# A graph layer on one core: two slots change places, the start's TensorE work lies at the head of the loop, and the first turn turns its own x

## The chip, the cores and the metric

The kernel runs on one core of a Trainium2 chip. The metric is the device time of one execution in microseconds, median of several runs. TensorE (PE, with its weight loads as PEld), VectorE (DVE), ScalarE (ACT), GpSimd (POOL) and SyncE (SP, which issues most transfers) each run their own list of instructions in order and wait for each other by semaphores.

## The reference

Inputs: 12,500 nodes of 128 numbers (`x`), 412,500 edges of 48 numbers, sorted by the node they point at (`dst`), one graph vector of 64 and a two-layer network. Cut to what is computed:

```python
agg = jax.ops.segment_sum(edge_attr_48, dst, num_segments=12500)
h = jnp.maximum(_layernorm(x, axis=-1), 0.0)
c = jnp.concatenate([h, agg, u], axis=1)          # 128 + 48 + 64; u is the same row for all nodes
y = x + jax.nn.relu(c @ W1 + b1) @ W2 + b2
```

So for each node the edges that point at it are added up, and a small network is run on node, sum and graph vector. All is float32.

## The kernel before

**The work.** A chunk is 128 x 6 edges, a group four chunks (3,072 edges). A turn of the loop takes eleven groups and 1,024 nodes, which are two halves A and B of 512; there are twelve turns, and a rest behind the loop. The edges of a turn lie in six slots (`SLOTS`, line 39) of one or two groups, each with its own tile `e`, its one-hots `oh`, its sums `ss` and its places `pl`. Per slot VectorE compares the ids within a chunk with 0 to 27 (`onehots`, line 769), TensorE multiplies edges by these one-hots (`add_up`, line 810: `su`, 24 products per group, two matmuls each in the trace) into bank S0 or S1, ScalarE copies the sums out (`ss`), and TensorE adds them to the turn's nodes by a second one-hot (`place`, line 825: `pc`, banks ax and ay). ScalarE copies these out as `ags`.

**The network.** In the next turn the sums meet their nodes: `layer_e` (ha, line 893) adds `ags` x W1 to what `layer_x` (hh, line 888) of the turn before left in four banks (pt, po, ph0, ph1), ScalarE applies relu (hi), and `second` (w2, line 910) multiplies by W2, which VectorE adds to the held x (ho). `hh` needs the normed, transposed x: VectorE takes statistics (`stats`, `variance`), ScalarE a square root (`root`, sq), VectorE finishes `sc` and `sh`, ScalarE makes xn (`norm`, eight activations), TensorE transposes (`turn`, tu), ScalarE copies (hT). So in turn i the statistics and norms of the x of turn i+1 are made, and that x is transposed in turn i+1. An x tile is loaded again when it has been normed and copied into `hold`. Results are kept in `hold` and stored behind the loop.

**The order.** Nothing schedules at run time: `prologue`, `body` and `epilogue` write operations into a list, `Flow.order` derives the waits from what each reads and writes, and each engine runs its own in the written order. SyncE issues loads in that order too, and blocks where a slot is still being read. In the first turn what belongs to a turn before is left out (`f.skip`).

**TensorE's code.** For the other engines the start is straight code ahead of a loop. For TensorE `Flow.run` writes one loop by hand and puts the start's work inside, in a branch behind the code of the turn. A counter `j` tells where to go. Before, in round 1 it branches from the head over `if0` and `if1` to `work0` (ids: five `of`, ten triples of transposes `td`), in round 2 over `if0` to `work1` (transposes of the first x, `su5` for the rows ahead of the first turn, `bi`, and `hh` of the first x), and in round 3 the first turn begins. In the text's listing a row's xN counts products of the program.

**The start.** SyncE loads two of five pieces of dst, both halves of x, the other pieces, then e and weights. VectorE turns ids into differences (`dst_1`, lines 677 to 681, three buffers), TensorE transposes them (`dst_2`, line 694), ScalarE copies them to `rel` (line 695).

Of the kernel before, what the change touches and what calls it, by code (L numbers as in the profile page):

```python
# [10 lines left out]
F32 = mybir.dt.float32  # L11
# [7 lines left out]
P = 128  # L19
# [19 lines left out]
SLOTS = [(1, 6), (2, 7), (3, 8), (4, 9), (5,), (10, 11)]  # L39
NS = len(SLOTS)  # L40
HI = 64

# [12 lines left out]
class Flow:  # L55
# [146 lines left out]
    def run(self):  # L202
# [96 lines left out]
        pe.reg_add(j, j, 1)  # L299
        either(n, "if0", "first", "IS_GE")  # L300
        part("first", "head", False)
        at, k = "first", 0
        for skip, some in groupby(own, lambda o: o["name"] in self.skip):
            some = list(some)
            if not skip:
                for o in some:
                    repeat(o, None)
                continue
            part(f"if{k}", at if k else "head")
            at = f"if{k}"  # L310
            either(n + 1, f"brief{k}", f"whole{k}", "IS_GE")
            part(f"whole{k}", at, False)
            for o in some:
                repeat(o, None)
            pe.br(f"pe_both{k}")
            part(f"brief{k}", at, False)
            if k:
                either(2, "work0", "brief1a")
                work(0, "brief1", todo[:most])
# [3 lines left out]
            else:  # L323
                either(2, "if1", "brief0a", "IS_GE")
                part("brief0a", "brief0", False)
                either(n, "work1", "both0")
                work(1, "brief0a", todo[most:])
            part(f"both{k}", at, False)
            at = f"both{k}" if k else "if0"
            k += 1  # L330
# [3 lines left out]
        part("after", "if1", False)  # L334
# [159 lines left out]
def kernel(  # L494
# [106 lines left out]
    mf = [const.tile([P, P // CG], F32, name=f"mf{k}") for k in range(NB)]  # L601
# [70 lines left out]
    def dst_1(b):  # L672
        rows, n, g0 = dst_shape(b)
        d = di[b]
        k = f"di{b}"
        src = [k] + ([k + "r", k + "s"] if b == NB - 1 else [])
        op("DVE", f"fc{b}", src, [f"fc{b}"], lambda i: [nc.vector.tensor_copy(fc[b][:rows], d[:rows, 0:1])])
        k = b % DF
        op("DVE", f"df{b}", src + [f"fc{b}"], [f"df{k}"], lambda i: [
            nc.vector.tensor_scalar(df[k][:rows], d[:rows], fc[b][:rows], (V - 1) / 2, OP.subtract, OP.subtract)])  # L680
        op("DVE", f"mf{b}", [f"fc{b}", "m4"], [f"mf{b}"], lambda i: [nc.vector.tensor_scalar(mf[b][:rows], m4[:rows], fc[b][:rows], None, OP.mult)])

    def dst_2(b):
        rows, n, g0 = dst_shape(b)
        ob, ok = agg[0], "of"
        op("PE", f"of{b}", [f"mf{b}", "aq"], [ok], lambda i: [
            nc.tensor.matmul(ob[:, g0:g0 + n], aq[:rows].rearrange("c k n -> c (k n)"), mf[b][:rows, :n], start=True, stop=True, skip_group_check=True)])
        dv = df[b % DF].rearrange("c (p t) -> c t p", t=T)
        rv = rel[:, :, b * P:b * P + rows]
        for t0 in range(0, T, 3):  # L690
            key, bk = (("PT", pt), ("PH0", ph[0]), ("PO", po))[(2 * b + t0 // 3) % 3]
            pv = bk[:, :3 * P].rearrange("p (t c) -> p t c", t=3)
            op("PE", f"td{b}.{t0}", [f"df{b % DF}", "ident"], [key],
               lambda i, t0=t0, pv=pv: [nc.tensor.transpose(pv[:, t, :rows], dv[:rows, t0 + t, :], ident[:rows, :rows]) for t in range(3)])
            op("ACT", f"cd{b}.{t0}", [key], [f"rel{b}.{t0}"], lambda i, t0=t0, pv=pv: [nc.scalar.copy(rv[:, t0:t0 + 3], pv[:, :, :rows])])  # L695

# [146 lines left out]
    def stats(k):  # L843
        op("DVE", f"st{k}", [f"x{k}"], [f"st{k}"], lambda i: [nc.vector.bn_stats(st[:, k * R + r], xt[k][:, r]) for r in range(R)])  # L844
# [32 lines left out]
    def turn(k, bk, key, front=""):  # L877
        pv = bk.rearrange("p (r c) -> p r c", r=R)
        op("PE", f"tu{front}{k}", [f"xn{k}", "ident"], [key], lambda i: [nc.tensor.transpose(pv[:, r], xn[k][:, r], ident) for r in range(R)])  # L879
        op("ACT", f"hT{front}{k}", [key], [f"hT{k}"], lambda i: [nc.scalar.copy(hT[k], pv)])  # L880
# [24 lines left out]
    def layers(fn, front=""):  # L905

        for a, k, key, bk in middle:
            fn(f"{front}{k}.{a}", key, bk.rearrange("p (r c) -> p r c", r=R), k, a)
# [36 lines left out]
    def prologue():  # L945
        f.at = -1
        load_dst(0)
        load_dst(1)
        for k in (A, B):
            load_x(k, 1, "SP")  # L950
        for b in range(2, NB):
            load_dst(b)
        load_dst(NB - 1, True)
        dma("SP", "le5.1", [], ["e5.1"], e[5][:, CG:], edge_attr[:GE].rearrange("(c p t) d -> p c (t d)", p=P, t=T))
        load_e(0, 1, 0)
        dma("SP", "lw1h", [], ["w1h"], w1h, W1[0:D])
        load_e(0, 1, 1)
# [5 lines left out]
        for s in range(2, NS):  # L963
# [6 lines left out]
            out=ident, in_=ident, compare_op=OP.not_equal, fill=1.0, base=0, pattern=[[-1, P]], channel_multiplier=1), ["ident"])  # L970
        pool("s5z", ["ssf"], lambda: nc.gpsimd.memset(ssf[:, 0], 0.0))
# [28 lines left out]
        dst_1(0)  # L1000
        dst_2(0)
        dst_1(1)
        stats(A)
        stats(B)
        variance()
        root()
        dst_2(1)
        dst_1(2)
        shift()
        norm(A, (0, 1))  # L1010
        dst_2(2)
        norm(A, (2, 3))
        dst_1(3)
        dst_2(3)
        norm(B, (0, 1))
        dst_1(4)
        dst_2(4)
        norm(B, (2, 3))
# [8 lines left out]
        op("ACT", "ssf", ["bk1"], ["ssf", "bk1"], lambda i: [nc.scalar.copy(ssf[:, 1], agg[1][:, :DE])])  # L1027
        fetch(1)
        onehots(0)
        onehots(1)  # L1030
        op("PE", "bi", ["w1u", "u", "u1", "b1"], ["of"], lambda i: [
            nc.tensor.matmul(agg[0][:, NG + a:NG + a + 1], w1u[:, a * P:(a + 1) * P], u, start=True, stop=True, skip_group_check=True) for a in range(NH)])
        layers(layer_x, "f")
# [3 lines left out]
        onehots(2)  # L1037
# [12 lines left out]
    def body(it):  # L1050
# [30 lines left out]
        norm(A, (0, 1))  # L1081
        turn(B, po, "PO")
        norm(A, (2, 3))
# [7 lines left out]
        layers(layer_x)  # L1091
        onehots(4)
# [62 lines left out]
    f.cut = "tuf0"  # L1155
    f.skip = {f"{n}{k}.{a}" for n in ("ha", "hi", "hh") for k in (A, B) for a in range(NH)} | {f"{n}{k}" for n in ("tu", "hT", "w2", "ho") for k in (A, B)}
# [38 lines left out]
```

## Time and profile before

| | |
|---|---|
| time, median of 3 runs (range) | 265.36 us (264.72 to 265.43) |
| the profiled execution, its span | 266.01 us, 264.1 us |
| busy: TensorE, VectorE, ScalarE | 236.4, 227.9, 132.8 us |
| moved | 94.40 MB, mean 357 GB/s |
| first matmul; first turn of the loop; second turn | 9.78; 28.66; 49.46 us |
| end of the last turn; of the span | 245.92; 264.1 us |

In a row of a timeline stand the start, the length, the engine, the line and operation, what is written and read, how often, and in brackets the idle time before it and what ended it; "issue" means that the profile shows nothing it waited for. A row of windows gives a stretch, its length, the busy time of each engine with its instructions, the granted TensorE clock (1.00 is full), the busy share of the DMA engines and GB/s. A row of a DMA queue gives packets, MB and its share of 16 engines' time. A turn here is always a pass through the loop's body.

### The profile page before, as it was taken

To read this page: it belongs to the slowest core of one execution; us is meant where nothing else is said; L and a number is where in the kernel's file an instruction comes from. 1 tells how busy PE (TensorE), PEld (TensorE's weight loads), DVE (VectorE), ACT (ScalarE), POOL (GpSimd) and SP (SyncE) were. 2 spreads that over 40 slices of the span, in tenths; PEclk is the share of its full clock that TensorE was granted. 3 is DMA by queue.
4 is the path that set the end of the run, shared out by engine and by line. 5 is a ranking of instruction groups with operands and counts; after the bars stand their busy time and mean duration, and the time that the engine had idled before them with its cause. 6 is when DMAs were issued, how large, how long until landed. Compare 5 with 4: busy or idle time off the path is not lost.

```text
span 264.1 us, 17108 instructions
## 1 busy us (share of the span) xinstructions
PE 236.4 (90%) x7537; PEld 184.6 (70%) x7538; DVE 227.9 (86%) x548; ACT 132.8 (50%) x315; POOL 4.3 (2%) x18
## 2 busy tenths in 40 slices
PE   0589922999999999999999999999999999999991
PEld 0575612886796778867967877679679677886780
DVE  5598695799998998998989989989999899899951
ACT  2291115375572673754736826537467367375520
POOL 6000000000000000000000000000000000000000
PEclk9985885899999999999999999999999999999999
DMA  6999999899999999999999999999999999969922
GB/s 209 345 344 386 347 382 384 255 382 390 365 390 393 377 390 392 390 390 392 390 392 391 391 392 391 390 392 390 392 390 390 392 390 390 367 248 380 358 96 76
DMA packets 79545, 94.40 MB, mean 357 GB/s; under 512 B 3228, under 2 KB 72842, under 8 KB 79528
## 3 DMA queue, kind: packets, MB, share of 16 engines
q1 hardware_dynamic: 76318, 88.60, 94.4%
q10 hardware_dynamic: 3114, 5.52, 5.5%
q8 instruction: 10, 0.16, 0.3%
q0 software_dynamic: 96, 0.07, 0.1%
q14 instruction: 7, 0.06, 0.1%
HBM read 87.77 MB, written 6.40 MB: 357 GB/s over the span
## 4 chain that ended last, share of the span: by engine, by line
PE 85%; issue 6%; DVE 3%; ACT 2%; DMA 2%; SPq 0%
PE s L815 28%; PE ph L914 16%; PE ph L891 8%; PE ax L837 7%; PE pt L896 4%; PE pt L891 4%; PE po L891 4%; PE ph L896 4%; PE pt L879 2%; PE po L879 2%; DMA holda<-in_dst_dram 2%; PE ax L801 1%; DVE far L709 1%; ACT rel L695 1%; ACT xnb L868 1%
## 5 line engine op out<-in xcount | busy, mean ns | idle before, releaser
L761 DVE TENSOR_TENSOR oh<-iota_v,rel_i 128x1344 f32<-128x1344 f32 (+1 forms) x78 | 110.9, 1438 | 11.1 <-PE s L815 10.7
L815 PEld LDWEIGHTS s<-e,oh 128*28 128x28 f32 x6336 | 71.0, 108 | 29.2 <-issue 28.6
L815 PE MATMUL s<-e,oh 128*28 128x48 f32 x6336 | 76.2, 208 | 10.8 <-issue 10.8
L819 ACT COPY ss<-s 128x96 f32<-128x96 f32 (+1 forms) x72 | 17.0, 236 | 63.8 <-PE s L815 62.7
L767 DVE TENSOR_SCALAR pl<-iota_w,off_i 128x186 f32<-128x186 f32 x112 | 26.5, 315 | 0.5
L868 ACT ACTIVATE xna<-xa,sh,sc 128x128 f32<-128x128 f32 x52 | 25.7, 494 | 1.3 <-issue 0.4
L868 ACT ACTIVATE xnb<-xb,sh,sc 128x128 f32<-128x128 f32 x52 | 25.5, 490 | 1.3
L914 PE MATMUL ph<-w,hida 128*128 128x128 f32 x192 | 23.5, 276 | 0.0
L914 PEld LDWEIGHTS ph<-w,hida 128*128 128x128 f32 x192 | 22.4, 192 | 0.3 <-issue 0.3
L914 PE MATMUL ph<-w,hidb 128*128 128x128 f32 x176 | 21.4, 275 | 0.0
L914 PEld LDWEIGHTS ph<-w,hidb 128*128 128x128 f32 x176 | 20.5, 192 | 0.0
L837 PE MATMUL ax<-pl,ss 128*48 128x186 f32 (+1 forms) x120 | 20.1, 316 | 0.0
L837 PE MATMUL ay<-pl,ss 128*48 128x186 f32 (+1 forms) x120 | 20.1, 316 | 0.0
L837 PEld LDWEIGHTS ax<-pl,ss 128*48 128x48 f32 x120 | 14.1, 126 | 3.8
L844 DVE BATCH_NORM_STATS2 st<-xa 128x6 f32<-128x128 f32 x52 | 11.3, 285 | 4.2 <-DMA xa<-in_x_dram 4.2
L837 PEld LDWEIGHTS ay<-pl,ss 128*48 128x48 f32 x120 | 14.1, 126 | 0.0
L896 PE MATMUL po<-ags,w1a 48*128 48x512 f32 x24 | 13.5, 641 | 0.0
L896 PE MATMUL pt<-ags,w1a 48*128 48x512 f32 x24 | 13.5, 641 | 0.0
L805 ACT COPY ssf<-ss 128x96 f32<-128x96 f32 x12 | 3.3, 272 | 20.1 <-PE ay L801 20.1
L891 PE MATMUL pt<-hta,w1h 128*128 128x512 f32 x24 | 13.3, 638 | 0.0
L891 PE MATMUL ph<-hta,w1h 128*128 128x512 f32 x24 | 13.2, 631 | 0.0
L891 PE MATMUL po<-htb,w1h 128*128 128x512 f32 x24 | 13.1, 631 | 0.0
(140 smaller groups left out, 313.5 us busy)
## 6 DMA issues: line engine op xcount, KB each, us to landing
e<-in_edge_attr_dram SPq DMA_DIRECT2D x133, 576.0 KB, 7.7
out_dram<-holda SPq DMA_DIRECT2D x12, 256.0 KB, 3.1
out_dram<-holdb SPq DMA_DIRECT2D x11, 256.0 KB, 3.0
xa<-in_x_dram ACTq DMA_DIRECT2D x10, 256.0 KB, 5.3
xb<-in_x_dram ACTq DMA_DIRECT2D x10, 256.0 KB, 5.8
holda<-in_dst_dram SPq DMA_DIRECT2D x4, 384.0 KB, 6.0
e<-in_edge_attr_dram SPq DMA_DIRECT2D x1, 720.0 KB, 5.8
xa<-in_x_dram SPq DMA_DIRECT2D x2, 256.0 KB, 7.2
```

The costliest lines, as they stand in the source:

```text
L761: op("DVE", f"oh{name}", reads + ["iota_v"], [f"oh{name}"], lambda i: [nc.vector.tensor_tensor(ov, iota_v[:, None, None, :].to_broadcast([ ...
L767: nc.vector.tensor_scalar(out[:, j], iota_w, o[j], None, OP.is_equal) for j in range(len(o))])
L805: op("ACT", "ssf", ["ss5"], ["ssf"], lambda i: [nc.scalar.copy(ssf, ss[5])])
L815: nc.tensor.matmul(S[k][NV * c:NV * c + V, j * DE:(j + 1) * DE], o[:, (j * CG + c) * T + t], ev[:, j * CG + c, t * DE:(t + 1) * DE], start ...
L819: op("ACT", f"ss{name}", [f"S{k}"], [f"ss{name}"], lambda i: [nc.scalar.copy(sv.rearrange("p j d -> p (j d)"), S[k][:, :m * DE])])
L837: out.append(nc.tensor.matmul(agg[bk][h:h + DE, at:at + w], sv[:, j], pv[:, j, frm:frm + w], start=bk in fresh and bk not in seen, stop=Tr ...
L844: op("DVE", f"st{k}", [f"x{k}"], [f"st{k}"], lambda i: [nc.vector.bn_stats(st[:, k * R + r], xt[k][:, r]) for r in range(R)])
L868: nc.scalar.activation(xn[k][:, r], xt[k][:, r], AF.Relu, bias=sh[:, c + r:c + r + 1], scale=sc[:, c + r:c + r + 1])])
L879: op("PE", f"tu{front}{k}", [f"xn{k}", "ident"], [key], lambda i: [nc.tensor.transpose(pv[:, r], xn[k][:, r], ident) for r in range(R)])
L891: nc.tensor.matmul(o, w1h[:, a * P:(a + 1) * P], src, start=first, stop=False, skip_group_check=True)])
L896: nc.tensor.matmul(o, w1a[h:h + DE, a * P:(a + 1) * P], ag[k // 2][h:h + DE], start=False, stop=True, skip_group_check=True)])
L914: nc.tensor.matmul(ov[:, r], hid[k][:, a, r], w2[:, a], start=(a == 0), stop=(a == NH - 1)) for r in range(R) for a in range(NH)])
```

## The change

- Slots 3 and 4 change places in `SLOTS`: slot 3 now has one group, slot 4 two. Slot 4's sums move behind `layer_x`.
- TensorE's start is cut into three pieces of work, which lie right behind the head of the loop. Even rounds (2, 4, 6) run one each; odd rounds run none and branch through the code of the turn: round 3 as far as `if0`, round 5 as far as `if1`, round 7 as far as `tail`, always back to the head. Round 8 is the first turn.
- The first turn now runs its own transposes, hT and `hh`; the start's copies of them are gone, and `f.skip` leaves out only ha, hi, w2, ho. In every turn both transposes stand ahead of both w2.
- SyncE loads all of dst first, then two pieces of e, then x. VectorE does all of dst, the first one-hots, and then the statistics of x. Five `of` products become one, over a shared `mf_all`.
- Six products of the identity with itself (`warm`) end the third piece of work.

TensorE's list, in the loop from slot 2 on, before (s0, s1: banks; e, oh: slot tiles):

```order
L815 MATMUL s0_65<-e2_76,oh2_88 28x48 x48
L815 MATMUL s1_66<-e3_77,oh3_89 28x48 x48
L815 MATMUL s0_65<-e4_78,oh4_90 28x48 x24
L273 UNCONDITIONAL_BRANCH
L280 COMPARE_AND_BRANCH
L879 MATMUL pt_69<-ident_131,xna_108 128x128 x4
L914 MATMUL ph0_70<-w2_127,hida_114 128x128 x8
L879 MATMUL po_72<-ident_131,xnb_109 128x128 x4
L914 MATMUL ph1_71<-w2_127,hidb_115 128x128 x8
L891 MATMUL pt_69<-hta_110,w1h_124 128x512
```

and now:

```order
L841 MATMUL s0_65<-e2_76,oh2_88 28x48 x48
L841 MATMUL s1_66<-e3_77,oh3_89 28x48 x24
L905 MATMUL pt_69<-ident_131,xna_108 128x128 x4
L905 MATMUL po_72<-ident_131,xnb_109 128x128 x4
L274 UNCONDITIONAL_BRANCH
L283 COMPARE_AND_BRANCH x3
L346 UNCONDITIONAL_BRANCH
L940 MATMUL ph0_70<-w2_127,hida_114 128x128 x8
L940 MATMUL ph1_71<-w2_127,hidb_115 128x128 x8
L274 UNCONDITIONAL_BRANCH
L283 COMPARE_AND_BRANCH
L917 MATMUL pt_69<-hta_110,w1h_124 128x512
```

The transposes left the skipped part, one group of slot 3 and all of slot 4 left the place ahead of them; slot 4 (two groups) now follows the four products with w1h.

ScalarE's list at the start, from the second copy of ids on, before:

```order
L695 COPY rel<-ph_70 128x3x128
L857 ACTIVATE sc<-sm,eps 128x8
L695 COPY rel<-po 128x3x128
L695 COPY rel<-pt 128x3x128
L868 ACTIVATE xna<-xa,sh,sc 128x128 x2
```

and now, from the last copies of ids on (`ssf<-ay` waits for the sums of TensorE's third piece):

```order
L717 COPY rel<-po 128x3x26
L717 COPY rel<-pt 128x3x26
L1035 COPY ssf<-ay 128x48
L883 ACTIVATE sc<-sm,eps 128x8
L894 ACTIVATE xna<-xa,sh,sc 128x128 x4
L894 ACTIVATE xnb<-xb,sh,sc 128x128 x4
```

The square root and the norms of the first x moved behind all copies of ids and behind `ssf`.

The diff, cut to its core:

```diff
-SLOTS = [(1, 6), (2, 7), (3, 8), (4, 9), (5,), (10, 11)]
+SLOTS = [(1, 6), (2, 7), (3, 8), (5,), (4, 9), (10, 11)]
+WARM = 6
...
-        most = [o["name"] for o in todo].index(self.cut)
+        a, b = ([o["name"] for o in todo].index(v) for v in self.cuts)
...
-            if n:
+            if n == 2:
                 ahead("PE")
             pe.br("pe_head")
 
-        n = 3
+        n = 8
         turns = hi - lo + 1
         pe.reg_mov(j, 0)
         zero("PE")
         part("head", None)
         pe.reg_add(j, j, 1)
+        either(n, "early", "gate", "IS_GE")
+        part("early", "head", False)
+        either(2, "work0", "early1", "IS_EQ")
+        work(0, "early", todo[:a])
+        part("early1", "early", False)
+        either(4, "work1", "early2", "IS_EQ")
+        work(1, "early1", todo[a:b])
+        part("early2", "early1", False)
+        either(6, "work2", "early3", "IS_EQ")
+        work(2, "early2", todo[b:])
+        part("early3", "early2", False)
+        either(2, "head", "early4")
+        part("early4", "early3", False)
+        pe.br("pe_gate")
+        part("gate", "head", False)
         either(n, "if0", "first", "IS_GE")
...
+            if k == 0:
+                either(n + 1, "brief0", "whole0", "IS_GE")
...
+                part("brief0", at, False)
+                either(4, "head", "brief0a")
+                part("brief0a", "brief0", False)
+                either(n, "if1", "both0", "IS_GE")
+                part("both0", at, False)
+            else:
+                either(n + 1, "brief1", "whole1")
+                part("brief1", at, False)
+                either(6, "head", "brief1a")
                 part("brief1a", "brief1", False)
+                either(n, "tail", "brief1b")
+                part("brief1b", "brief1a", False)
                 ahead("PE", True)
-                pe.br("pe_both1")
...
+                pe.br("pe_tail")
+                part("whole1", at, False)
+                for o in some:
+                    repeat(o, None)
+                part("tail", at)
+                either(n, "head", "both1")
+                part("both1", "tail", False)
...
+    def middles():
+        op("PE", "of", [f"mf{b}" for b in range(NB)] + ["aq"], ["of"], lambda i: [
+            nc.tensor.matmul(agg[0][:, :NG], aq.rearrange("c k n -> c (k n)"), mf_all[:, :NG], start=True, stop=True, skip_group_check=True)])
...
-        load_dst(0)
-        load_dst(1)
-        for k in (A, B):
-            load_x(k, 1, "SP")
-        for b in range(2, NB):
+        for b in range(NB):
             load_dst(b)
         load_dst(NB - 1, True)
         dma("SP", "le5.1", [], ["e5.1"], e[5][:, CG:], edge_attr[:GE].rearrange("(c p t) d -> p c (t d)", p=P, t=T))
         load_e(0, 1, 0)
+        for k in (A, B):
+            load_x(k, 1, "SP")
+        load_e(0, 1, 1)
...
-        turn(A, S[0], "S0", "f")
-        turn(B, S[1], "S1", "f")
...
+        op("PE", "warm", ["ident"], ["PH1"], lambda i: [
+            nc.tensor.matmul(ph[1][:, :P], ident, ident, start=True, stop=True, skip_group_check=True) for _ in range(WARM)])
         fetch(1)
         onehots(0)
+        stats(A)
+        stats(B)
+        variance()
+        root()
         onehots(1)
...
-        layers(layer_x, "f")
...
-        add_slots(4)
         onehots(1)
         turn(A, pt, "PT")
+        turn(B, po, "PO")
         second(A, ph[0], "PH0", -1)
         add_b(A, 1)
-        norm(A, (0, 1))
-        turn(B, po, "PO")
-        norm(A, (2, 3))
+        norm(A)
...
         layers(layer_x)
+        add_slots(4)
         onehots(4)
...
-    f.cut = "tuf0"
-    f.skip = {f"{n}{k}.{a}" for n in ("ha", "hi", "hh") for k in (A, B) for a in range(NH)} | {f"{n}{k}" for n in ("tu", "hT", "w2", "ho") for k in (A, B)}
+    f.cuts = "td2.0", "su5"
+    f.skip = {f"{n}{k}.{a}" for n in ("ha", "hi") for k in (A, B) for a in range(NH)} | {f"{n}{k}" for n in ("w2", "ho") for k in (A, B)}
```

More of the change, by code (lines that the diff above doesn't have):

```diff
@@ L299, in run @@
         pe.reg_add(j, j, 1)
+        either(n, "early", "gate", "IS_GE")
[13 more added lines that the diff above has]
+        part("gate", "head", False)
         either(n, "if0", "first", "IS_GE")
-        part("first", "head", False)
+        part("first", "gate", False)
         at, k = "first", 0
@@ L333, in run @@
         either(n + turns, "first", "after")
-        part("after", "if1", False)
+        part("after", "both1", False)
         self.straight(end)
@@ L600 @@
     fc = [const.tile([P, 1], F32, name=f"fc{k}") for k in range(NB)]
-    mf = [const.tile([P, P // CG], F32, name=f"mf{k}") for k in range(NB)]
+    mf_all = const.tile([P, NB * P // CG], F32)
+    mf = [mf_all[:, k * P // CG:(k + 1) * P // CG] for k in range(NB)]
     vv = const.tile([P, NB * P // CG], F32)
@@ L680, in dst_1 @@
             nc.vector.tensor_scalar(df[k][:rows], d[:rows], fc[b][:rows], (V - 1) / 2, OP.subtract, OP.subtract)])
[L681 removed]
+        op("DVE", f"mf{b}", [f"fc{b}", "m4", "mfz"], [f"mf{b}"], lambda i: [nc.vector.tensor_scalar(mf[b][:rows], m4[:rows], fc[b][:rows], None, OP.mult)])
     def dst_2(b):
         rows, n, g0 = dst_shape(b)
[L685 to L687 removed]
         dv = df[b % DF].rearrange("c (p t) -> c t p", t=T)
@@ L875, in add_b, with turn @@
             nc.vector.tensor_tensor(held(k, i, n), xt[k], b2_sb[:, None, :].to_broadcast([P, R, D]), OP.add)])
-    def turn(k, bk, key, front=""):
+    def turn(k, bk, key):
         pv = bk.rearrange("p (r c) -> p r c", r=R)
-        op("PE", f"tu{front}{k}", [f"xn{k}", "ident"], [key], lambda i: [nc.tensor.transpose(pv[:, r], xn[k][:, r], ident) for r in range(R)])
-        op("ACT", f"hT{front}{k}", [key], [f"hT{k}"], lambda i: [nc.scalar.copy(hT[k], pv)])
+        op("PE", f"tu{k}", [f"xn{k}", "ident"], [key], lambda i: [nc.tensor.transpose(pv[:, r], xn[k][:, r], ident) for r in range(R)])
+        op("ACT", f"hT{k}", [key], [f"hT{k}"], lambda i: [nc.scalar.copy(hT[k], pv)])
     def sums_out(k, eng="ACT"):
@@ L999, in prologue @@
         op("DVE", "c3", ["iota_v"], ["iota_v"], lambda i: [nc.vector.tensor_scalar(iota_v, iota_v, 0.5, None, OP.mult)])
[L1000 to L1009, printed above, removed]
-        norm(A, (0, 1))
-        dst_2(2)
-        norm(A, (2, 3))
[L1013 to L1018, printed above, removed]
+        for b in range(NB):
+            dst_1(b)
+            dst_2(b)
+        middles()
         onehot(5, oh[5][:, q:], ["rel0.0", "rel0.3"], rel[:, :, :CG].rearrange("p t c -> p c t"))
-        turn(A, S[0], "S0", "f")
-        turn(B, S[1], "S1", "f")
         op("PE", "su5", ["oh5", "e5.1"], ["bk1"], lambda i: [
@@ L1075, in body @@
         shift()
[L1076 removed]
         onehots(1)
         turn(A, pt, "PT")
+        turn(B, po, "PO")
         second(A, ph[0], "PH0", -1)
         add_b(A, 1)
[L1081 to L1083 removed]
+        norm(A)
         onehots(2)
```

35 lines of the change are left out of this document (13 added, 22 removed).

## The prediction

> **What bounds the kernel now.** I first read the windows of the trace by stage, to see which turns of the loop are regular and which not.
>
> ```profile
> core 0: us, PE busy (x) PEld busy (x) DVE busy (x) ACT busy (x) POOL busy (x), PEclk, DMA share, GB/s
> 33.71:37.82 4.11, 0.00 (x2) 0.00 (x1) 3.93 (x12) 0.52 (x2) 0.00 (x0) 1.00 1.08 378
> 38.69:44.86 6.17, 0.00 (x0) 0.03 (x1) 4.82 (x5) 4.03 (x9) 0.00 (x0) 0.50 1.08 385
> 44.86:49.46 4.60, 4.60 (x125) 3.90 (x125) 1.56 (x1) 0.24 (x1) 0.00 (x0) 0.63 0.81 266
> 49.46:67.32 17.86, 17.86 (x616) 13.96 (x612) 16.67 (x39) 10.15 (x24) 0.00 (x0) 1.00 1.06 370
> 85.18:228.06 142.88, 142.88 (x4900) 111.67 (x4896) 133.34 (x312) 81.20 (x192) 0.00 (x0) 1.00 1.08 390
> ```
>
> From 49.46 on a turn takes 17.86 us (142.88 / 8 is 17.86 too): TensorE is never idle, VectorE works 16.67 of it, and the DMA engines are full at 390 GB/s. All three are close to their limit, so little can be won there. The first turn is another matter: 28.66 to 49.46 is 20.80 us for less work, and TensorE does nothing in 4.11 + 6.17 us of it. The timeline of TensorE shows where.
>
> ```profile
> 9.78 0.62 PE L687 MATMUL ax<-mf,aq 128*128 128x32 f32 x2 [9.78 <-issue]
> 10.21 0.88 PE L694 MATMUL pt<-ident,holda 128*128 128x128 f32 x3
> 10.89 0.84 PE L694 MATMUL ph<-ident,holda 128*128 128x128 f32 x3
> ...
> 22.33 2.05 PE L891 MATMUL pt<-hta,w1h 128*128 128x512 f32 x2
> ...
> 28.66 2.25 PE L815 MATMUL s<-e,oh 128*28 128x48 f32 x192
> 31.38 2.33 PE L815 MATMUL s<-e,oh 128*28 128x48 f32 x200 [0.48 <-issue]
> 37.82 0.87 PE L815 MATMUL s<-e,oh 128*28 128x48 f32 x40 [4.11 <-issue]
> 44.86 2.14 PE L815 MATMUL s<-e,oh 128*28 128x48 f32 x96 [6.18 <-issue]
> ```
>
> The 4.11 us gap lies inside one operation (240 matmuls, cut after 200), where the code has no wait. The DMA queues answer what is missing, asked for 28.6 to 49.4 and for 49.4 to 246:
>
> ```profile
> q8 instruction: 3, 0.05, 1.1%
> ...
> q1 hardware_dynamic: 61564, 70.17, 99.8%
> q10 hardware_dynamic: 2672, 4.85, 6.5%
> q14 instruction: 1, 0.01, 0.0%
> ```
>
> Queue q8 brings instructions, three packets in the first turn and none in the next eleven. I take them for TensorE's code, in blocks of 16 KB (0.16 MB in 10 packets, third part of the page):
>
> ```profile
> q8 instruction: 10, 0.16, 0.3%
> ```
>
> So TensorE waits for its own code on its first way through the loop, and what the way through once has brought stays. It also starts late, at 9.78, though VectorE had ids ready long before. VectorE's timeline, and SyncE's second load of x:
>
> ```profile
> 1.52 0.06 DVE L985 MEMSET zero<- 128x1 f32 x1 [1.39 <-SPq L1160]
> 4.17 0.62 DVE L680 TENSOR_SCALAR holda<-holda,fc 128x768 f32<-128x768 int32 x1
> 5.82 0.62 DVE L680 TENSOR_SCALAR holda<-holda,fc 128x768 f32<-128x768 int32 x1
> 26.01 0.45 SPq L613 DMA_DIRECT2D xb<-in_x_dram  x1
> 32.48 0.88 DVE L844 BATCH_NORM_STATS2 st<-xa 128x6 f32<-128x128 f32 x4 [2.37 <-DMA xa<-in_x_dram]
> 33.27 0.86 DVE L844 BATCH_NORM_STATS2 st<-xb 128x6 f32<-128x128 f32 x4
> 34.67 0.17 DVE L854 SCALAR_TENSOR_TENSOR sm<-sm 128x8 f32<-128x8 f32 x1
> 41.19 2.32 DVE L761 TENSOR_TENSOR oh<-iota_v,rel_i 128x1344 f32<-128x1344 f32 x2
> 47.06 1.56 DVE L761 TENSOR_TENSOR oh<-iota_v,rel_i 128x1344 f32<-128x1344 f32 x1 [3.55 <-PE s L815]
> 49.58 0.45 DVE L780 TENSOR_SCALAR plf<-iota_w,off_i 128x46 f32<-128x46 f32 x2 [0.96 <-PE ay L801]
> ```
>
> This is the second view that decides: VectorE in the first turn cannot go on before the second x has landed (32.48), and from there waits for TensorE only 3.55 + 0.96 us.
>
> **The change, part by part.** *The start.* The first work lies by the head of the loop and needs no far jump, so TensorE starts at 4.9 instead of 9.78. Transposes come 0.68 us apart (10.21, 10.89), the second pair waits for the ids of 5.82 + 0.62: done at about 7.9. Then a round only branches through the code and meets a block that is not there. A fetch costs between 4.11 (the part of one that showed) and 8.2 us (9.78 less 1.5, where VectorE's first row stands); the nearest row is the second gap, 6.18, with 0.87 us of work since the gap before: 6.2 to 7.05. I take 6.2. Round 3 ends at 14.1; the remaining transposes, six groups of at most 0.68 us and one product in place of five, end by 18.5; the next block, asked for at 14.1, comes at 20.3; the third piece of work runs from 20.3 to about 24; the block after it, asked for at 20.3, comes at 26.5. The first turn starts at 26.5 instead of 28.66. The eight slow matmuls of the old start (22.33 to 28.66) are gone; they come back in the turn. The first x now stands behind 1.2 MB more of e, 3 us at 390 GB/s; nobody needs its norms before the first turn's transposes after 30, and VectorE makes one-hots meanwhile. Were that cover gone, ScalarE's chain below would start up to 3 us later.
>
> *ScalarE.* The square root of the first x now stands behind the copy of ssf, which waits for the third piece's sums (20.3 + 1.1). So the root is done at 21.9, VectorE's shift at 22.5, eight norms of 0.51 us (2.07 for 4, next rows) at 26.6. The second load of xb waits for them: 26.6 instead of 26.01, so the second x lands 0.6 us later and VectorE's variance ends at 35.4 instead of 34.84.
>
> ```profile
> 39.29 2.07 ACT L868 ACTIVATE xna<-xa,sh,sc 128x128 f32<-128x128 f32 x4 [0.36 <-issue]
> ...
> 127.45 0.30 ACT L857 ACTIVATE sc<-sm,eps 128x8 f32<-128x8 f32 x1
> 128.39 0.59 ACT L880 COPY hta<-pt 128x512 f32<-128x512 f32 x1 [0.36 <-PE pt L879]
> ...
> 127.69 0.66 PE L879 MATMUL pt<-ident,xna 128*128 128x128 f32 x4
> ...
> 64.29 1.23 PE L815 MATMUL s<-e,oh 128*28 128x48 f32 x96
> 67.32 2.25 PE L815 MATMUL s<-e,oh 128*28 128x48 f32 x192
> ```
>
> *The first turn* now turns its own x, and there ScalarE's root for the next x stands ahead of the copies hT. Root (0.3) and first copy (0.59) end at 36.4; until then the matmuls with w1h wait, which nobody waited for before. Behind them: four pairs 3.52 us (132.20 to 135.72 below), two slots' sums, four groups, 2.2 (2.25 for 192 matmuls, 0.55 a group), the rest of the turn 3.03 - 1.1 = 1.94 (64.29 to 67.32, less two groups): 44.0 at full clock. But TensorE has sat idle before that. Seven groups of sums (3.85) and the transposes (0.5 to 0.66 each four) from 26.5 end between 31.5 and 36.4 by the clock, so idle time is 0 to 4.9 us; after 4.11 us idle the row 38.69:44.86 has the clock at 0.50, and 44.86:49.46 took 4.60 against 3.03. That is 1.6 us; the eight matmuls at half clock cost 6.33 against 3.52, 2.8 us. Bounds 0 and 2.8, I take 2.0: the second turn starts at 46.0 instead of 49.46. VectorE allows that: from 35.4 the same 8.7 us as from 34.84 to 43.5 and one more one-hot of 1.5, so 45.6.
>
> The Trainium skill's page "TensorE: Matmul & The Clock Gate" (The HAM clock gate) has half the clock after one idle window of about 3.4 us and full clock after one busy one; the trace agrees (idle 4.11, then 0.50), and by it the loss is an estimated 1.7 to 3.4 us.
>
> *The regular turn.* Slots 3 and 4 change places; the work stays. What moves is a wait:
>
> ```profile
> 132.20 1.02 PE L891 MATMUL pt<-hta,w1h 128*128 128x512 f32 x2
> 132.85 0.68 DVE L916 TENSOR_TENSOR holdb<-ph,holdb 128x512 f32 x1
> 134.77 1.02 PE L891 MATMUL ph<-htb,w1h 128*128 128x512 f32 x2
> 135.72 1.23 PE L815 MATMUL s<-e,oh 128*28 128x48 f32 x96
> 137.02 1.56 DVE L761 TENSOR_TENSOR oh<-iota_v,rel_i 128x1344 f32<-128x1344 f32 x1 [0.65 <-PE s L815]
> ```
>
> The last pair (134.77) overwrites what VectorE reads until 133.53: 1.24 us of room. Two groups of sums now come after it, so it starts 1.1 us sooner. And slot 4's one-hots now wait for sums late in the turn: these end at 14.83 (64.29 - 49.46; two groups more, two less ahead), VectorE follows 0.2 later, and two one-hots of at most 1.56 us end at 18.1, against 17.86 + 0.12 (49.58 - 49.46) where VectorE goes on now. Of 0.14 us of room, 0.02 to 0.14 is left; I put the turn at 17.86. Loads stay hidden: the DMA engines are full anyway, and new e for slot 4 has over 16 us.
>
> **Sum.** The profiled execution took 266.01 us (its span 264.1); 46.0 - 49.46 = -3.5, the other eleven turns and the tail as before: 262.5. It lay 0.65 over the median of the runs: 261.9.
>
> **The rivals.**
> *The rounds do not keep code* (slower). The old start ran work in a block beside those it later fetched again, so a jump there left nothing of use. If blocks walked through by branches are dropped too, the first turn starts at 26.5, has eleven groups of sums (6.0), transposes (1.0), pairs (3.5) and the rest (1.9), 12.4 us, with 10.3 of gaps and 1.6 of slow clock: 50.8, 1.3 later than now, 266.7. It decides as soon as both gaps come back. Against it: the old short rounds went back to the head and forward again, and the way through the first two blocks had no gap.
> The Trainium skill's "Runtime: NRT & Kernel Launch" (Instruction fetch mechanics) speaks for it: a branch out of a window of 2 blocks of 16 KiB forces a fetch. The trace disagrees at least for the loop: no packet of q8 in eleven turns.
> *Slow fetches*: at 8.2 us each the third piece starts at 24.3, the second x is 4.6 us later than before, the matmuls wait until 40.4 and the turn ends at 49.6: 265.4, no change. For it: the queue is full; against it: 6.18.
> *VectorE sets the pace*: no slow clock and no delay of x, VectorE is through at 34.84 + 8.7 + 1.5 = 45.0 instead of 49.58, 4.6 us are won and the time is 260.8; with x landing a microsecond sooner 259.8. Against it: the idle time ahead of the copies.
> *The reordered turn is longer*: the 0.1 us of room fails and each turn waits 0.3 us, as VectorE's 0.30 to 0.65 us waits are: 11 x 0.3 gives back 3.3: 265.2.
>
> **How the numbers follow.** Forecast 0.48, VectorE's pace 0.18, slow fetches 0.14, longer turns 0.11, code not kept 0.09. About 0.3% (0.8 us) is what a measurement here can tell. Faster: forecast and VectorE's pace whole, 0.08 of slow fetches (7.05 us each moves x by 2.3 us, the turn's end to 47.8 and the time to 263.7) and 0.04 of longer turns: 0.78. Slower: the last, and 0.01 of longer turns: 0.10. Same: 0.12. The range goes from VectorE's best, 259.8, to 264.8, which leaves out the code not kept, most of longer turns and the worst of the fetches.
>
> **What would show it.** Right: first matmul near 5; three or four q8 packets before 27 and no gap inside a sum of the first turn; a wait for hT near 31 to 36, with the clock at 0.50 after it; the second turn at 46, regular turns of 17.86. Wrong: gaps of 4 us and more by "issue" in the first turn; the second x later than 35; turns over 18.0; VectorE waiting nowhere in the first turn.

## The result: 261.12 us, and the profile after

| | before | changed |
|---|---|---|
| time, median of 4 runs each (range) | 265.04 us (264.68 to 265.43) | 261.12 us (260.79 to 262.73) |
| the profiled execution, its span | 266.01 us, 264.1 us | 260.79 us, 258.9 us |
| second turn starts; last turn ends | 49.46; 245.92 us | 44.16; 240.68 us |
| eleven turns; what follows | 196.46; 18.18 us | 196.52; 18.22 us |

The ratio is 0.9864, with a 95% interval of 0.982 to 0.9908. The forecast was 261.9 us.

Between the two profiled executions 5.22 us lie, and the table says where: 5.30 are won before the second turn, 0.06 and 0.04 are lost in the turns and behind them. The medians lie only 3.92 us apart. The profiled execution of before was 0.97 us over its median, that of the changed kernel 0.33 us under its own, so 1.3 us of the 5.22 belong to these two executions.

The windows of the changed kernel, cut where TensorE's work changes:

```profile
core 0: us, PE busy (x) PEld busy (x) DVE busy (x) ACT busy (x) POOL busy (x), PEclk, DMA share, GB/s
14.77:17.45 2.68, 0.01 (x1) 0.04 (x2) 2.58 (x12) 0.00 (x0) 0.00 (x0) 1.00 1.09 387
28.85:35.06 6.21, 0.00 (x1) 0.00 (x0) 3.92 (x19) 0.82 (x3) 0.00 (x0) 0.68 1.08 391
35.06:40.11 5.05, 5.05 (x9) 2.03 (x9) 5.01 (x7) 3.81 (x9) 0.00 (x0) 0.71 1.09 390
79.89:222.81 142.92, 142.92 (x4900) 111.53 (x4896) 132.23 (x313) 81.25 (x192) 0.00 (x0) 1.00 1.08 390
```

The regular turn is what it was (142.92 / 8 is 17.87). The two gaps of the old first turn, 4.11 and 6.18 us, are gone. In their place stands one of 6.21 us, and the matmuls with w1h behind it take 5.05 us at a mean clock of 0.71. TensorE's timeline tells what each stretch waits for:

```profile
4.84 0.93 PE L716 MATMUL pt<-ident,holda 128*128 128x128 f32 x3 [4.84 <-DVE holda L705]
17.45 1.18 PE L1031 MATMUL ay<-e,oh 128*28 128x48 f32 x48 [2.68 <-issue]
22.87 2.88 PE L841 MATMUL s<-e,oh 128*28 128x48 f32 x192 [0.53 <-issue]
26.09 1.74 PE L841 MATMUL s<-e,oh 128*28 128x48 f32 x144 [0.34 <-issue]
35.06 2.08 PE L917 MATMUL pt<-hta,w1h 128*128 128x512 f32 x2 [6.21 <-ACT hta L906]
40.11 2.24 PE L841 MATMUL s<-e,oh 128*28 128x48 f32 x192
44.16 2.25 PE L841 MATMUL s<-e,oh 128*28 128x48 f32 x192
```

The first turn starts at 22.87, and what TensorE waits for in it is no longer code but ScalarE's copy hT. ScalarE's timeline shows why that copy is late, and VectorE's what else ends at the same moment:

```profile
21.53 2.06 ACT L894 ACTIVATE xnb<-xb,sh,sc 128x128 f32<-128x128 f32 x4
34.23 0.30 ACT L883 ACTIVATE sc<-sm,eps 128x8 f32<-128x8 f32 x1 [6.15 <-DVE sm L880]
34.44 0.57 ACT L906 COPY hta<-pt 128x512 f32<-128x512 f32 x1
```

```profile
31.86 0.87 DVE L870 BATCH_NORM_STATS2 st<-xa 128x6 f32<-128x128 f32 x4 [2.15 <-DMA xa<-in_x_dram]
44.34 0.44 DVE L806 TENSOR_SCALAR plf<-iota_w,off_i 128x46 f32<-128x46 f32 x2
```

The copy stands behind the root (34.23), the root waits for VectorE's variance, and that for the second x, which lands at 31.86. From there VectorE has no idle time at all until the new turn's places at 44.34. So one late transfer holds both engines: TensorE by way of hT, VectorE directly, and they reach the end of the turn within 0.2 us of each other. The issues of SyncE (start and duration of the stretch that it spends on them) say why it is late:

```profile
14.75 8.83 SPq L638 DMA_DIRECT2D e<-in_edge_attr_dram  x7
23.70 1.34 SPq L638 DMA_DIRECT2D xa<-in_x_dram  x1
25.15 0.38 SPq L638 DMA_DIRECT2D xb<-in_x_dram  x1
```

Seven loads of edges stand ahead of x and take 8.83 us to issue, 1.3 us each, about what 576 KB take at 390 GB/s (1.5). The profile shows no semaphore that SyncE waits for in this stretch, so I read it as held up by a full queue. The norms of the first x end at 23.59 (21.53 + 2.06), so they are not what xb (25.15) waits for.

### The profile page after: what moved, and what is told of

The parts are those of the page before. It is cut to its first block, busy times and chain, and to the rows that moved or that the text cites. A ratio compares the mean times of both kernels' runs of the same rounds, so it can differ in the third digit from the quotient of the medians.

```text
span 258.9 us, 17106 instructions
## 1 busy us (share of the span) xinstructions
PE 235.5 (91%) x7541; PEld 184.2 (71%) x7542; DVE 226.3 (87%) x548; ACT 133.7 (52%) x315; POOL 4.3 (2%) x19
## 4 chain that ended last, share of the span: by engine, by line
PE 81%; SPq 8%; DVE 4%; DMA 3%; issue 1%; ACT 0%; DVEq 0%
PE s L841 26%; PE ph L940 16%; SPq L638 8%; PE ph L917 8%; PE ax L863 6%; PE pt L917 4%; PE pt L922 4%; PE po L917 4%; PE ph L922 4%; DMA xa<-in_x_dram 3%; PE pt L905 2%; PE po L905 2%; DVE far L735 1%; PE ax L827 1%; DVE oh L787 1%
## 5 line engine op out<-in xcount | busy, mean ns | idle before, releaser
L787 DVE TENSOR_TENSOR oh<-iota_v,rel_i 128x1344 f32<-128x1344 f32 x78 | 110.8, 1436 | 12.5 <-PE s L841 12.0
L841 PEld LDWEIGHTS s<-e,oh 128*28 128x28 f32 x6336 | 70.6, 107 | 19.3 <-issue 18.7
L845 ACT COPY ss<-s 128x96 f32<-128x96 f32 x72 | 17.0, 236 | 54.8 <-PE s L841 54.4
L793 DVE TENSOR_SCALAR pl<-iota_w,off_i 128x186 f32<-128x186 f32 x112 | 26.5, 312 | 0.5
L863 PE MATMUL ax<-pl,ss 128*48 128x186 f32 (+1 forms) x120 | 19.5, 309 | 0.0
L863 PE MATMUL ay<-pl,ss 128*48 128x186 f32 (+1 forms) x120 | 19.4, 309 | 0.0
L863 PEld LDWEIGHTS ax<-pl,ss 128*48 128x48 f32 x120 | 12.7, 123 | 2.8
L927 ACT ACTIVATE hida<-pt,bias 128x512 f32<-128x512 f32 x12 | 8.2, 687 | 9.2 <-PE pt L922 9.2
L863 PEld LDWEIGHTS ay<-pl,ss 128*48 128x48 f32 x120 | 12.7, 123 | 0.0
```

Source lines behind the costliest of these rows:

```text
L787: op("DVE", f"oh{name}", reads + ["iota_v"], [f"oh{name}"], lambda i: [nc.vector.tensor_tensor(ov, iota_v[:, None, None, :].to_broadcast([ ...
L793: nc.vector.tensor_scalar(out[:, j], iota_w, o[j], None, OP.is_equal) for j in range(len(o))])
L841: nc.tensor.matmul(S[k][NV * c:NV * c + V, j * DE:(j + 1) * DE], o[:, (j * CG + c) * T + t], ev[:, j * CG + c, t * DE:(t + 1) * DE], start ...
L845: op("ACT", f"ss{name}", [f"S{k}"], [f"ss{name}"], lambda i: [nc.scalar.copy(sv.rearrange("p j d -> p (j d)"), S[k][:, :m * DE])])
L863: out.append(nc.tensor.matmul(agg[bk][h:h + DE, at:at + w], sv[:, j], pv[:, j, frm:frm + w], start=bk in fresh and bk not in seen, stop=Tr ...
```

## Experiments

Each ratio, with its 95% interval, is to the kernel before, run beside it on the same chip.

**The same kernel again.** No edit.

> The changed kernel once more, unedited, to have a second profile of it and times on the same chip as the edits. If the stages of the first profile are typical: second turn of the loop near 44.2 us, regular turns of 17.86, time 261.1 within 0.8. If the profile taken first was a lucky one (it lay 0.33 us under the median of its runs, the one of the kernel before 0.97 over its own): second turn between 44.5 and 45.2, all else the same.

261.99 us (0.9921, 0.9886 to 0.9955). TensorE's timeline of this execution:

```profile
34.66 2.07 PE L917 MATMUL pt<-hta,w1h 128*128 128x512 f32 x2 [7.07 <-ACT hta L906]
40.88 2.24 PE L841 MATMUL s<-e,oh 128*28 128x48 f32 x192
44.94 2.25 PE L841 MATMUL s<-e,oh 128*28 128x48 f32 x192
```

and one row of VectorE's:

```profile
42.17 3.03 DVE L787 TENSOR_TENSOR oh<-iota_v,rel_i 128x1344 f32<-128x1344 f32 x2 [1.16 <-PE s L841]
```

hT was there 0.4 us sooner than in the first profile, and the second turn still started 0.78 us later: the four pairs with w1h took 6.22 us in place of 5.05, and here VectorE waits 1.16 us for TensorE's sums. When the clock rises behind the same wait is the main difference between the two profiles, so the start of the second turn varies by this much from one execution to the next.

**hT ahead of the root.**

```diff
-        root()
-        shift()
         onehots(1)
         turn(A, pt, "PT")
         turn(B, po, "PO")
+        root()
+        shift()
```

> ScalarE copies hT ahead of the square root for the next x, in each turn; VectorE's shift moves behind slot 1's one-hots. Theory A, the forecast's mechanism (TensorE waits for hT because the root stands ahead of it, and this wait sets the end of the first turn): the wait of 6.21 us ahead of the matmuls with w1h shrinks below 1 us, and the second turn starts 2 to 5 us sooner, time 256 to 259. Theory B (VectorE sets the pace, its one-hots of slot 4 end at 40.03, TensorE reaches them at 40.11): the wait only moves behind the matmuls with w1h, the second turn starts at 44.0 to 44.4, time unchanged within 0.4.

264.52 us (1.0001, 0.9965 to 1.0036): as slow as the kernel before, so neither theory had it; the second turn started at 45.86. Timelines of TensorE and ScalarE:

```profile
28.42 1.12 PE L917 MATMUL pt<-hta,w1h 128*128 128x512 f32 x2 [0.24 <-ACT hta L906]
44.44 0.54 PE L863 MATMUL ax<-pl,ss 128*48 128x186 f32 x1 [8.89 <-ACT ss L845]
```

```profile
41.12 2.06 ACT L894 ACTIVATE xnb<-xb,sh,sc 128x128 f32<-128x128 f32 x4
44.15 0.38 ACT L845 COPY ss<-s 128x96 f32<-128x96 f32 x2 [0.97 <-ACT xnb L894]
```

The wait for hT is gone (0.24), as theory A had it, and a wait of 8.89 us stands further down: ScalarE's copies of the last sums come behind the norms, and the norms hang on the same second x. Part of the wait is the edit's own: it also puts VectorE's shift behind slot 1's one-hots, so the norms start 3.76 us behind the start of the root (39.14 against 35.38), where in the changed kernel it was 2.30 (36.53 against 34.23). Taking one consumer of x out of TensorE's way only brings up the next. The turns cost the rest: the ten from 64.37 to 244.41 take 18.00 us each in place of 17.87, and as in the last experiment below the weights of the last pair with w1h wait longer for VectorE's ho B (0.7 us a turn in place of 0.5).

**The second x early.** The change moves nothing but SyncE's order.

```diff
-        for s in range(2, NS):
-            for k in (0, 1):
-                if (s, k) != (5, 1) and k < len(SLOTS[s]):
-                    load_e(s, 1, k)
+        load_e(2, 1)
+        load_e(3, 1)
...
-        load_e(5, 1, 1)
...
         load_x_next(2, "SP")
+        load_e(4, 1)
+        load_e(5, 1)
```

> SyncE issues the second load of x ahead of the first loads of slots 4 and 5 in place of behind them; nothing else. Theory B (the second x, landed at 31.86, holds VectorE up by 2.15 us, and from there VectorE sets the pace): x lands near 27, the 2.15 us go, the second turn starts near 42.0, time 259.0. Theory A gives the same, since the root hangs on the same x. Rival C (the DMA engines are full, so what is moved ahead is taken from the edges behind it): e of slots 4 and 5 comes too late or later turns wait for loads, and the time stays within 0.5 of 261.1.

258.56 us (0.9804, 0.9744 to 0.9865), 3.4 us under the changed kernel beside it (261.99), where 2.1 were expected. SyncE's issues, then VectorE and TensorE:

```profile
20.41 0.35 SPq L638 DMA_DIRECT2D xa<-in_x_dram  x1
22.37 0.35 SPq L638 DMA_DIRECT2D xb<-in_x_dram  x1
```

```profile
28.32 0.86 DVE L870 BATCH_NORM_STATS2 st<-xa 128x6 f32<-128x128 f32 x4
```

```profile
31.51 1.99 PE L917 MATMUL pt<-hta,w1h 128*128 128x512 f32 x2 [3.66 <-ACT hta L906]
40.90 2.25 PE L841 MATMUL s<-e,oh 128*28 128x48 f32 x192
```

x is issued when its tiles are free (its norms end at 20.3 and 22.3), VectorE no longer waits for it, hT comes 3.5 us sooner than in the first profile. The edges of slots 4 and 5 come no later than they are needed, and the turns stay at 17.87: rival C is out. Run again beside the walk experiment below it gave the same ratio:

> The kernel with the second load of x issued early, unedited once more, to stand beside the next one on the same chip: second turn at 40.9 within 0.5, time 258.6 within 0.6.

259.21 us (0.9804, 0.9769 to 0.9840); in that execution the second turn started at 42.58, past the range I gave, and the four pairs took 6.65 us.

**No walks.** One number: the odd rounds go back to the head from every j under 8.

```diff
-        either(2, "head", "early4")
+        either(n, "head", "early4")
```

> The odd rounds of TensorE's start go straight back to the head and walk through no code; the code's layout stays the same word for word. Theory W (the walks bring blocks of code that are kept): the first turn of the loop starts up to 3 us sooner (the 2.68 us gap ahead of the third piece goes), but gaps inside the first turn come back, 4 to 6 us each at two or three places, of which the wait for hT (6.21 us) hides one: second turn at 48 to 52, time 265 to 269. Rival (the start in line is enough, each block is asked for in time on the way through): no such gap, second turn at 44.2 or sooner, time within 0.5 of 261.1.

262.02 us (0.9915, 0.9879 to 0.9951): no different from the changed kernel (261.99). TensorE's timeline:

```profile
19.16 2.86 PE L841 MATMUL s<-e,oh 128*28 128x48 f32 x192
27.34 2.30 PE L841 MATMUL s<-e,oh 128*28 128x48 f32 x103 [4.32 <-issue]
35.79 2.07 PE L917 MATMUL pt<-hta,w1h 128*128 128x512 f32 x2 [4.58 <-ACT hta L906]
```

A gap of 4.32 us does come back, but the first turn starts 2.5 us sooner (19.16 against 21.64 in the second profile), and the wait for hT, shorter by as much, covers the rest. The second turn of this execution started at 46.03, 1.09 us later than in the second profile of the changed kernel, because x landed 1.12 us later (32.57 against 31.45); over twelve runs each the medians do not differ. Only one gap came, where theory W had two or three. So walk and no walk cannot be told apart here, and I thought the late x was the reason:

**No walks, with x early.** Both edits above.

> The second load of x early and the odd rounds without a walk, together. Theory M (the walk does bring code in time, and alone it made no difference only because the late second x held the first turn up for longer than the missing blocks do): with x early the wait for hT is 3.7 us in place of 7, and the 4.3 us gap and the requests behind it show: second turn at 42 to 45, 1 to 4 us slower than the kernel with the walk. Theory N (the walk is not needed: each block is asked for in time once the first work lies in line): second turn at 40.9, the same time within 0.6.

259.26 us (0.9803, 0.9767 to 0.9839), the same as with the walks (259.21). Theory M falls as it was put: the shorter wait for hT did not bring the gaps out, and the second turn started at 42.34 (42.58 with the walks). TensorE's timeline:

```profile
25.69 1.31 PE L841 MATMUL s<-e,oh 128*28 128x48 f32 x103 [2.43 <-issue]
31.86 2.06 PE L917 MATMUL pt<-hta,w1h 128*128 128x512 f32 x2 [3.83 <-ACT hta L906]
```

What the runs had in common stands in the DMA records of the trace, the starts of the packets of queue q8 (16 KB of instructions each):

```
                        first turn from   packets of q8 begin at (us)
before                  28.66             5.2  6.1  12.9  23.2  35.3  41.9  45.4
changed                 22.87             5.6  12.7  19.4  25.3  42.7
no walks                19.16             5.6  24.9  31.1  37.2  44.3
x early, no walks       19.56             6.0  23.2  29.3  35.1  42.9
```

Without walks the packets of the first turn come one after another, and the first of them 3.7 to 6.6 us after the turn has begun. Up to the last packet of a row they are 5.7 to 6.6 us apart. The last one comes 3.5 us behind in the kernel before, where the DMA engines moved 266 GB/s, and 7.1 and 7.8 us behind in the two runs without walks. With the walks the chain starts 10 us before the first turn (12.7 against 22.87). So I formed theory C: what matters is when the chain starts, and an early first turn does for it what the walks do.

**A late first turn, with and without walks.** The products that end the third piece wait for a load, in the second kernel with the edit of the walks beside it.

```diff
-        op("PE", "warm", ["ident"], ["PH1"], lambda i: [
+        op("PE", "warm", ["ident", "e3.0"], ["PH1"], lambda i: [
```

> The changed kernel, with the products of the identity that end the third piece waiting for the load of slot 3's edges (landed at 24.9 in the changed kernel), so that the first turn of the loop starts late, near 28, as in the kernel before (28.66). The walks through the code stay. Theory C (blocks of code come one after another, 6.2 us apart, from the moment TensorE first enters them; the walk starts this chain before the first turn): no gap inside the first turn, its sums and transposes end near 34, hT is there at 35.5, second turn at 44 to 45: no slower than the changed kernel (261.1 to 262.0).

> The same late start without the walks. Theory C: the chain starts only at 28, so its blocks come near 34 and 40 and a gap of about 4 us comes back inside the sums and another of some us behind the transposes, as in the kernel before; too late for the wait for hT to cover them: second turn at 46 to 48, time 263.5 to 266. Rival N (the walk does nothing, whenever the first turn starts): the same second turn and time as with the walks, within 0.6.

With walks 261.36 us (0.9880, 0.9825 to 0.9935), without 266.44 us (1.0078, 1.0041 to 1.0116): 5.1 us apart, and the second is slower than the kernel before. Without walks the second turn (49.37) and the time lie past the ranges I gave. TensorE and VectorE with walks, then TensorE without:

```profile
29.46 6.11 PE L841 MATMUL s<-e,oh 128*28 128x48 f32 x336 [1.13 <-issue]
36.83 1.13 PE L917 MATMUL pt<-hta,w1h 128*128 128x512 f32 x2 [0.24 <-ACT hta L906]
44.52 2.25 PE L841 MATMUL s<-e,oh 128*28 128x48 f32 x192
```

```profile
32.07 0.87 DVE L870 BATCH_NORM_STATS2 st<-xa 128x6 f32<-128x128 f32 x4 [2.50 <-DMA xa<-in_x_dram]
44.70 0.44 DVE L806 TENSOR_SCALAR plf<-iota_w,off_i 128x46 f32<-128x46 f32 x2
```

```profile
33.73 1.31 PE L841 MATMUL s<-e,oh 128*28 128x48 f32 x103 [1.31 <-issue]
39.99 1.60 PE L917 MATMUL pt<-hta,w1h 128*128 128x512 f32 x2 [3.93 <-issue]
49.37 2.25 PE L841 MATMUL s<-e,oh 128*28 128x48 f32 x192
```

With the walks the first turn could start 6.6 us late and cost nothing: its sums run through without a gap. Without them the gaps are back by "issue", the last one ahead of the matmuls with w1h at 39.99, where nothing covers it. The queue of instructions in the two first turns (29.46 to 44.52, and 28.28 to 49.37) has one packet and four:

```profile
q8 instruction: 1, 0.02, 0.5%
```

```profile
q8 instruction: 4, 0.07, 1.3%
```

With walks hT is no longer late, and the four pairs run at full clock (36.83 to 40.46). TensorE waits only 0.24 us between 29.46 and 44.52, so here its own late start sets the second turn. VectorE is busy from 32.07 to 44.70 and gets there 0.2 us behind it, so this run doesn't tell what VectorE alone would allow.

**x early in the kernel before.** The same move of SyncE's loads, in the old code.

> The kernel before with the same move on SyncE: the second load of x ahead of the first loads of slots 4 and 5; nothing else. Theory (in the kernel before, TensorE's missing code sets the end of the first turn and VectorE waits for it, 3.55 and 0.96 us): x lands 4 to 5 us sooner than 32.48, the second turn stays at 49 to 49.7, time within 0.6 of the kernel before. Rival (the second x sets the end of the first turn in both kernels): second turn 2.5 to 4.5 us sooner, time 260.5 to 262.5.

264.51 us (0.9999, 0.9966 to 1.0031): no difference, as the theory had it; the second turn started at 48.72, a little before the range I gave. VectorE takes the statistics 2.9 us sooner and waits the longer for TensorE (5.34 us in place of 3.55), whose gaps stay. TensorE's timeline, then VectorE's:

```profile
36.86 0.63 PE L815 MATMUL s<-e,oh 128*28 128x48 f32 x40 [3.56 <-issue]
43.80 2.14 PE L815 MATMUL s<-e,oh 128*28 128x48 f32 x96 [6.32 <-issue]
```

```profile
29.61 0.87 DVE L844 BATCH_NORM_STATS2 st<-xa 128x6 f32<-128x128 f32 x4
46.00 1.56 DVE L761 TENSOR_TENSOR oh<-iota_v,rel_i 128x1344 f32<-128x1344 f32 x1 [5.34 <-PE s L815]
```

So the change has moved the bound of the first turn from TensorE's code to the second x; the same edit is worth nothing on one side of it and 3.4 us on the other.

**The old slots.** `SLOTS` and the place of slot 4's sums as before, the rest of the change kept.

```diff
-SLOTS = [(1, 6), (2, 7), (3, 8), (5,), (4, 9), (10, 11)]
+SLOTS = [(1, 6), (2, 7), (3, 8), (4, 9), (5,), (10, 11)]
...
         shift()
+        add_slots(4)
         onehots(1)
...
         layers(layer_x)
-        add_slots(4)
```

> The changed kernel with the slots as they were before (two groups in slot 3, one in slot 4, slot 4's sums ahead of the transposes), all else of the change kept. My theory (the reorder is worth nothing in the regular turn, 17.86 us with both orders, and in the first turn it only shifts sums from one side of the wait for hT to the other): regular turns of 17.86, second turn between 43.6 and 45.0, time within 0.6 of the changed kernel's 261.1 to 262.0. Rival (the reorder carries part of the gain): regular turns over 17.95 or the second turn past 46, time above 263.

262.21 us (0.9915, 0.9883 to 0.9948), the same as the changed kernel, and turns of 17.86: the reorder is worth nothing that can be measured. The second turn started at 45.70, past the range I gave. Its profile has one thing I had not expected, in the timelines of TensorE and VectorE:

```profile
22.08 1.18 PE L1031 MATMUL ay<-e,oh 128*28 128x48 f32 x48 [8.19 <-issue]
```

```profile
23.75 0.20 DVE L887 RECIPROCAL sc<-sc 128x8 f32<-128x8 f32 x1 [5.45 <-ACT sc L883]
```

With two more groups of sums ahead of `if1` the walk of round 5 goes further, and TensorE stands 8.19 us in place of 2.68. VectorE then waits 5.45 us for the root behind `ssf`, and the norms, and with them the second x, come later. Here both loads of x are issued as the norms end (26.35 and 28.31): that is the wait which the forecast placed in the changed kernel. I read the longer stop as one block more on the way; the trace shows no block's number, so that stays argued.

**One product of the identity in place of six.**

```diff
-WARM = 6
+WARM = 1
```

> One product of the identity in place of six at the end of the third piece. Theory (the first turn waits for code at its start and for hT later; the products only fill the first of the two waits): first turn starts within 0.6 us of the changed kernel's 21.6 to 22.9 or up to 2.4 sooner, second turn and time the same within 0.6. Rival (the products keep the granted clock up for the first sums): sums of the first turn slower, second turn more than 1 us later.

261.85 us (0.9897, 0.9858 to 0.9936), the same. The first turn starts at 21.22 behind a gap of 2.63 us by "issue": the products fill time in which code is on its way.

**x early and hT ahead of the root.** VectorE's order stays, ScalarE's root and norms go behind hT.

```diff
-        root()
-        shift()
-        onehots(1)
         turn(A, pt, "PT")
         turn(B, po, "PO")
+        root()
+        shift()
+        onehots(1)
```

> The second load of x early, and ScalarE copies hT ahead of the square root in each turn (VectorE's shift stays ahead of slot 1's one-hots). Theory B (with x early VectorE has hardly any idle time from 14 us on, so that it bounds the first turn): the wait for hT goes, TensorE waits for the sums of slot 4 behind the norms instead, second turn 39 to 41, and VectorE's places of the second turn start no sooner than 40.6; in the regular turn VectorE waits 0.45 us for the root, within its 1.1 of idle time, turns of 17.86: time 257 to 259. Rival (the later root and norms cost VectorE or the loads of x more than that): regular turns over 17.95 or a time above 259.5.

260.68 us (0.9868, 0.9813 to 0.9923): a miss, on the rival's side. The second turn did start at 40.31, but a regular turn now takes 18.08 us (144.67 / 8 below), and eight turns alone give back 1.75 us. The window of eight turns, the waits over five turns here, and one over eight of the changed kernel (us in total, times, longest):

```profile
59.09:203.76 144.67, 144.67 (x4900) 111.08 (x4896) 132.99 (x313) 81.13 (x192) 0.00 (x0) 1.00 1.08 391
```

```profile
PEld ph L917 <- DVE holdb L942: 3.9, 5, 0.8
...
DVE sc L887 <- ACT sc L883: 0.9, 5, 0.2
```

```profile
PEld ph L917 <- DVE holdb L942: 4.0, 8, 0.5
```

The weights of the last pair with w1h wait 0.8 us a turn for VectorE's ho B in place of 0.5. Of the room of 1.24 us at this place the reorder had taken 1.1, by the forecast's count; VectorE now waits 0.2 us a turn for the root (0.9 in five), and the turn is longer by 0.2. That these two waits make the turn longer is argued; TensorE shows no idle time in it.

The best kernel of the study is the changed one with the second x early: 258.56 and 259.21 us, 2% under the kernel before.

## Why the prediction was right, and where it was not

**The start in line**: 4.84 for the first transpose, 4.9 forecast.

**The rounds' fetches**: the size was about right, the moment of the first was wrong. I let round 3 ask for its block when the first work was done (7.9) and put the first turn at 26.5. The packets do come 5.9 to 7.1 us apart (5.6, 12.7, 19.4, 25.3), but the chain has its first packet at 5.6 while TensorE is still at its transposes, so that the work of the rounds lies beside it. Round 3, which I had ending at 14.1, cost nothing that shows: TensorE went on at 10.60, and the profile puts the 1.76 us before that down to VectorE's ids. What showed at the other two walks is 2.68 + 0.53 us, and of the 2.68 0.83 stays without walks. No packet starts inside the 2.68 us (14.77 to 17.45), so that this gap is a wait for code is argued. The first turn started at 22.87. Of these 3.6 us won over the forecast nothing reached the end: the wait for hT grew by them.

**The second x**: here the step was wrong in kind. I had its second load wait for the norms of the first x (26.6). The norms ended at 23.59, and x was held by SyncE's seven loads ahead of it, in the kernel before as well: there the same move let the statistics begin 2.9 us sooner. It landed at 31.86, VectorE's variance ended at 34.20 where I had 35.4.

**hT behind the root**: right as a mechanism. The matmuls with w1h started at 35.06 (36.4 forecast), most of the difference being that of x. The loss to the half clock was 5.05 less 3.52, 1.5 us, in one profile and 2.7 in the other, 2.0 forecast. The clock's share was 0.68 in the wait and 0.71 behind it. The Trainium skill's page "TensorE: Matmul & The Clock Gate" (The HAM clock gate) says that its window of 3.4 us runs free, so that where work starts within it is a matter of chance; 5.05, 6.22 and 6.65 us for the same four pairs agree.

**The second turn**: 44.16, and 44.94 in the second profile, against 46.0. By my own list a VectorE that waits nowhere in the first turn would speak against the forecast, and in the first profile it waits nowhere behind x. In the second profile it waits 1.16 us for TensorE, and in neither does TensorE wait for VectorE between hT and the second turn. So the forecast's chain, hT and the clock, was last or level, and the rival "VectorE sets the pace" was nearly the same case: both chains hang on the second x and end 0.2 us apart in the first profile, and the clock decides which is last. I had given 0.48 and 0.18 to two things that were hardly apart.

**The sum**: the time came out at 261.12 with 261.9 forecast because two errors met. The first turn was 1.84 us shorter than I had it; and I took the profiled execution to lie 0.65 over the median, while it lay 0.97 over it before and 0.33 under it after. That the time came within 0.8 us is in part luck.

**The regular turn** (17.86 forecast, 17.87): right in its length. The room ahead of the last pair, of which I left 0.02 to 0.14 us, is used up: its weights wait 0.5 us a turn for ho B (4.0 us in eight turns, above), but TensorE shows no idle time for it. The reorder neither costs nor gives anything; the rival of longer turns is out, though two experiments on ScalarE's order show how little room there is.

**Code not kept**: out. With walks and a late start the first turn ran without a gap. The Trainium skill's "Runtime: NRT & Kernel Launch" (Instruction fetch mechanics) has the next block fetched while the current one runs. The packet at 5.6 us agrees, with TensorE at its transposes; without walks the packet at 24.9 started only 1.9 us after TensorE had stopped (23.0). The same section's window of two blocks the trace does not bear out: with the late start the packets before the first turn (29.46) had come by 18.7, and only one more came in it, as none comes in eleven turns of the loop.

**What the gain is due to** I had put on the walks. The runs say: on an early first turn or on the walks, either being enough (262.02 and 261.36), and neither being there costs more than the kernel before (266.44). The early first turn in turn comes from the work in line (4.84 against 9.78) and from the eight matmuls with w1h that no longer stand ahead of it (6.33 us); these two were not tried apart.

## What to carry to other kernels

When the way through a loop is slow only the first time, look at when each block of code is asked for, as one looks at a load: start that chain early, under work that is there anyway. After such a change look for what holds both engines next; here it was one load that stood four places too far back among SyncE's issues, and moving it was worth nearly as much again (3.4 us). An engine's order that is changed for the first turn is paid for in every turn, so a gain at the start must be weighed against eleven times what it adds to one (0.2 us in the last experiment).

## What was not expected of the hardware

- Blocks of TensorE's instructions, 16 KB each, come one by one. Where several follow one another while the DMA engines are full (378 to 391 GB/s in the windows above), they are mostly 5.5 to 7.1 us apart (4.8 at the least, in the kernel with x early and hT ahead of the root), though a packet itself takes about 1 us. A first way through code that runs faster than that stops: 4.11 and 6.18 us in the kernel before.
- Branches that only pass through code bring it too, and it stays: with the late start the first turn has one packet of instructions behind the walks and four without them.
- SyncE's issues can take nearly as long as the transfers: seven loads of 576 KB took it 8.83 us with no semaphore to wait for, and the order of issue, not the wait on the tile, set when x came. Moved ahead of four loads, x was issued as soon as its norms had ended (20.41 and 22.37).
